# Attention of the last sequence: one more place for other matmuls in each step, 19 instead of 12 VectorE portions per pair

## The chip, the core and the metric

The kernel runs on one core of one Trainium2 chip. TensorE (PE) does matmuls and transposes into PSUM, VectorE (DVE) and ScalarE (ACT) read PSUM and work in SBUF, GpSimd (POOL) and SyncE (SP) mostly issue DMAs. The engines run their own instruction queues in order and wait for each other through semaphores. The metric is the device time of one execution in microseconds; the time before is the median of seven runs.

## The reference

Two layers, each with a sequence mixer and a mixture of experts, on 4 sequences of 1024 tokens of 256 values:

```python
x = L0_attn_x
x = x + _L0_attn_ref(_layernorm(x), ...)   # a gated recurrence (scan)
x = x + _L0_ffn_ref(_layernorm(x), ...)    # 8 experts, 2 per token
x = x + _L1_attn_ref(_layernorm(x), ...)   # causal attention, 16 heads of 64
x = x + _L1_ffn_ref(_layernorm(x), ...)    # 32 experts, 4 per token, and a shared one
return x
```

The change touches the third line, and the parts of the fourth that are computed beside it:

```python
att = jnp.einsum('bhcq,bhCq->bhcC', q, k) / d_query
att = jnp.where(causal, att, -jnp.inf)
p = jax.nn.softmax(att, axis=-1)
y = jnp.einsum('bhcC,bhCv->bhcv', p, v)
z = jnp.einsum('dvh,bhcv->bcd', W, y) * (math.sqrt(d_embed / d_value) / num_heads)
...
_, idx = jax.lax.top_k(scores + bias[None, :], K)      # routing of the fourth line
...
h = jax.nn.silu(jnp.einsum('ecd,edi->eci', xe, W1)) * jnp.einsum('ecd,edi->eci', xe, W3)
ye = jnp.einsum('eci,eid->ecd', h, W2)
```

## The kernel before

The attention runs sequence by sequence (`b` from 0 to 3), and in each over eight **pairs** of heads (`p`). A pair is cut into six **units**, the groups of 128-row query tiles in `GROUPS`: (0, 1), (2, 3), 4, 5, 6, 7. All 192 units form one pipeline in `run_steps`, whose order on all engines is written out by hand (`tc.manual_schedule()`): step `s` does the scores of unit `s` (L1452), the row minima on VectorE (L1466 and L1468) and the exponentials on ScalarE (L1481), the transposes of the exponentials of unit `s-1` (L1502, copied out at L1523), and the products with the values of unit `s-2` (`weighted`, L1538).

Between portions of `weighted`, each step has up to three **places** in the list `side` for a piece of other matmuls. Some hold what the attention itself needs: the queries, keys and values of the next pair (`queries`, `values`), and the softmax's divisors of the pair before (`norm_T`, `norm`). The others are called `"beside"` and take the next piece of a list of jobs, if that piece is due.

These jobs are Python generators (class `Beside`). `yield "pe"` announces a piece of matmuls and `yield "post"` the instructions that read its PSUM bank; `yield "dve"` ends a portion of VectorE work. A place calls `piece()`, which does something only when the job has come to a `"pe"`. At the end of each step, `beside.tick()` is called `TICKS[g]` times, and each call runs the job on to its next `yield`, if it stands at a `"dve"`. So places that meet a job at a `"dve"` stay empty, and so do calls that meet it at a `"pe"`. `TICKS` is (2, 3, 1, 3, 2, 1): 12 calls a pair.

In the last sequence (`b` = 3, pairs 24 to 31 when pairs are counted through all sequences) the jobs are, in order:

- `l3_out(2)`: the output projection of sequence 2, eight pieces `pz`, read at L1429;
- `l4_route(2, 0)` and `l4_route(2, 1)`: layer norm (L912, L913, the root in L884 to L897, `xn_l` at L919), transposes (`pt_l`, L931, copied by ScalarE at L935), gate scores (`pl_l`), top 4 (L947 to L967), positions (`pos_l`), rows (`row_l`, L1003), 16 scatters of rows to `xs_d` by GpSimd, the shared expert's hidden values (`s_l`), and the gates (L1034 to L1046);
- `l4_shared(2, h)`: the shared expert's second matmul (`sy`), added at L1061;
- `l4_experts_beside`: twelve tiles of experts' rows, two at a time. It makes the list of tiles (L1066 to L1097), loads rows (`room<-xs_d` on SP, L1112) and weights (`w_pairs<-e_w_dram` on POOL, L1107), then for two tiles each: rows on VectorE (L1117 to L1133), transposes `pta` (L1223, copied at L1225), hidden values `pea` (ScalarE L1210, VectorE L1211 and L1212), output `pya` (copied by ScalarE at L1195 into one buffer) and two scatters to `yt_d` (L859, POOL). Its weights go where the attention's weights of a pair stood, so it waits (`ready`) until those pairs are done: the first tiles until pair 28, from the second two on until pair 30.

All buffers in PSUM come from two pools: seven rotating banks (`ps_s`) for scores, transposes and pieces, and one for `weighted`.

After the last step, outside of the handwritten order, the output projection of sequence 3 (`pz`), what is left of the jobs, and `l4_route(3, 0)` and `l4_route(3, 1)` follow; their order on each engine is found by the scheduler:

```python
with tc.manual_schedule():
    run_steps()
drain(l3_out(B - 1, ps_s, "s"))
while beside.jobs or beside.job is not None:
    beside.step()
late = []
for h in range(2):
    drain(l4_route(B - 1, h, sm, ps_s, "s", late))
```

Then the last stage gathers the experts' rows of the first three sequences (`yg<-yt_d`, 24 loads on SP, L1729), adds them with their gates (L1736), runs the four tiles of experts that were not done beside (`ptg`, `eh`, `ey`, L1796 to L1820), gathers the last sequence's rows and stores. Its SBUF is that of the attention, so its loads come after the last reader of the attention's buffers.

Of the kernel before, what the change touches and what calls it, by code (L numbers as in the profile page):

```python
# [24 lines left out]
B, S, D = 4, 1024, 256  # L25
# [31 lines left out]
def block_kernel(  # L57
# [841 lines left out]
    def mm2(out, lhsT, rhs, start, stop):  # L899

        for par in range(2):
            r = slice(par * DH, (par + 1) * DH)
            nc.tensor.matmul(out[r], lhsT[:, r], rhs, start=start, stop=stop)  # L903
# [364 lines left out]
    with ExitStack() as ph:  # L1268
# [39 lines left out]
        def w_cols(k, p):  # L1308

            return w_pairs[:, p - 1, k] if p else w_pair0[:, k]  # L1310
# [4 lines left out]
        qs, ks, vs, ls, ys = {}, {}, {}, {}, {}  # L1315
        GROUPS = [(0, 1), (2, 3), (4,), (5,), (6,), (7,)]
        NG = len(GROUPS)
        TICKS = (2, 3, 1, 3, 2, 1)
        units = [(b, p, g) for b in range(B) for p in range(NP) for g in range(NG)]
        NU3 = len(units)  # L1320

# [31 lines left out]
        def values(b, p, hf):  # L1353

            held = {}

            def pe():
                held[0] = pv = ps_s.tile([P, HT, P], F32, name=f"pv_{b}_{p}_{hf}", tag="s")
                for q in range(HT):
                    i = hf * HT + q  # L1360
                    for c in range(NC_):
                        mm2(
                            pv[:, q, :], xTs[b][:, c, i * P : (i + 1) * P],
                            w_cols(2, p)[:, c, :], c == 0, c == NC_ - 1,
                        )

            def post():
                if hf == 0:
                    vs[b, p] = mid.tile([P, NT, P], F32, name=f"v_{b}_{p}", tag="v")
                nc.vector.tensor_copy(vs[b, p][:, hf * HT : (hf + 1) * HT, :], held[0])  # L1370

            return pe, post
# [47 lines left out]
        def l3_out(b, ps, tag):  # L1420
            y = [ys.pop((b, p)) for p in range(NP)]
            for i in range(NT):
                yield "pe"
                po = ps.tile([P, D], F32, name=f"pz_{b}_{i}", tag=tag)
                for p in range(NP):
                    mm2(po, y[p][:, i * P : (i + 1) * P], wo_t[:, p, :], p == 0, p == NP - 1)
                yield "post"

                nc.vector.scalar_tensor_tensor(  # L1429
                    x[b][:, i, :D], po, 0.0625, x[b][:, i, :D], ALU.mult, ALU.add  # L1430
                )
# [4 lines left out]
        def score_banks(u):  # L1436

            b, p, g = units[u]
            for par in range(2):
                for k, (i, kc) in enumerate(parts(u)):  # L1440
                    sps[u, k, par] = ps_s.tile(
                        [P, 512], F32, name=f"ps_{b}_{p}_{i}_{kc}_{par}", tag="s"
                    )
# [135 lines left out]
        beside = Beside()  # L1579
# [9 lines left out]
        def run_steps():  # L1589
            added, pending = [], []  # L1590
            at_pair = [0]
            inst = None
            for s in range(NU3 + 3):
                su = s if s < NU3 else None
                tu = s - 1 if 1 <= s <= NU3 else None
                vu = s - 2 if s >= 2 else None
                pair, g = divmod(s, NG)
                b, p = divmod(pair, NP)
                here, before = (b, p), divmod(pair - 1, NP)
                at_pair[0] = pair  # L1600
                ahead = divmod(pair + 1, NP)

                if g == 2 and p == 0 and 0 < b < B:
                    beside.jobs.append(l3_out(b - 1, ps_s, "s"))
                if (g, p) == ((2, 0) if b else (0, 4)) and b + 1 < B:
                    beside.jobs.append(l3_prepare_pieces(b + 1, sm, ps_s, "s"))
                if g == 2 and p == 0 and 0 < b < B:
                    beside.jobs += [l4_route(b - 1, h, sm, ps_s, "s") for h in range(2)]
                    beside.jobs += [l4_shared(b - 1, h, ps_s, "s") for h in range(2)]
                    if b == B - 1:  # L1610
                        beside.jobs.append(
                            l4_experts_beside(
                                sm, ps_s, "s", lambda j: w_pairs[:, j],
                                lambda j: at_pair[0] >= (B - 1) * NP + min(j, 5) + 1,
                            )
                        )

                side = []
                more = ahead[0] < B
                if g == 0:  # L1620
                    side = ["beside", "beside"]
                elif g == 1:
                    side = [norm_T(*before) if pair else "beside", "beside", "beside"]
                elif g == 2:
                    side = [
                        norm(*before, 0) if pair else None,
                        queries(*ahead, 0, False) if more else None,
                        norm(*before, 1) if pair else None,
                    ]
                elif g == 3:  # L1630
                    side = [queries(*ahead, 1, False), queries(*ahead, 0, True), "beside"] if more else []
                elif g == 4:
                    side = [queries(*ahead, 1, True), values(*ahead, 0), "beside"] if more else []
                else:
                    side = [values(*ahead, 1) if more else None, "beside", "beside"]
                side += [None] * (3 - len(side))

                def matmuls(k):

                    piece = side[k]  # L1640
                    if piece == "beside":
                        piece = beside.piece()
                    if piece is not None:
                        piece[0]()
                        pending.append(piece[1])

                def readers():
                    while pending:
                        pending.pop(0)()


                if tu is not None:
                    transposes(tu, 0)
                    transposed_out(tu, 0)
                if su is not None:
                    if g == 0:
                        ls[here] = sm.tile([P, NT, 2, 2], F32, name=f"l_{b}_{p}", tag="l")
                    score_banks(su)
                    scores(su, 0)
                    scores(su, 1)  # L1660
                if tu is not None:
                    transposes(tu, 1)
                if su is not None:
                    for par in range(2):
                        minimum(su, 0, par)
                        minimum(su, 1, par)
                    exps(su, 0, 0)
                    exps(su, 1, 0)
                if tu is not None:
                    transposed_out(tu, 1)  # L1670

                nb = GROUPS[units[vu][2]][-1] + 1 if vu is not None and vu < NU3 else 0
                cuts = [-(-nb // 2), nb, nb] if side[2] is None else [-(-nb // 3), -(-2 * nb // 3), nb]
                done = 0
                for k in range(3):
                    matmuls(k)
                    if cuts[k] > done:
                        weighted(vu, range(done, cuts[k]))
                        done = cuts[k]
                    if k == 0 and g == 0 and pair:  # L1680
                        norm_parts(*before)
                    if k == 0 and su is not None:
                        exps(su, 0, 1)
                        inst = exps(su, 1, 1)
                    readers()
                if nb:
                    weighted_out(vu)
                for _ in range(TICKS[g]):
                    beside.tick()
                if s % NG < NG - 1 and 2 <= s // NG * (NG - 1) + s % NG < TT + 2:  # L1690
                    l4_zeros(s // NG * (NG - 1) + s % NG - 2, inst)
                if 3 <= s < len(later) + 3:
                    added.pop(0)()
                if 1 <= s <= len(later):
                    added.append(later[s - 1](inst, sm))
            while pending:
                pending.pop(0)()

        with tc.manual_schedule():
            run_steps()  # L1700
# [13 lines left out]
    with ExitStack() as ph:  # L1714
# [107 lines left out]
        def l4_tiles(j0, n, lst):  # L1822
# [16 lines left out]
        more = nc.values_load(  # L1839
            flag_i[0:1, 0:1], min_val=0, max_val=1 << 20,  # L1840
            skip_runtime_bounds_check_because="a count, limited",
        )
# [87 lines left out]
```

## Time and profile before

| | us |
|---|---|
| median of 7 runs | 2043.13 (2040.6 to 2045.9) |
| the profiled execution, its own time | 2049.74 |
| its span in the profile | 2048.1 |
| layer 0, before the first score matmul | 609.2 |
| sequence 0, pairs 0 to 7 | 282.4 |
| sequence 1, pairs 8 to 15 | 339.9 |
| sequence 2, pairs 16 to 23 | 341.1 |
| sequence 3, pairs 24 to 31 and three more steps | 348.6 |
| the output projection of sequence 3 | 27.9 |
| from there to the end | 99.1 |

The stretches are read off the timeline: a sequence begins with its first score matmul (L1452). The places carry little in sequence 0, where there is nothing to do beside but the layer norm of sequence 1. How to read the rows that follow further down: a window's row has its bounds, its length, then for each engine the busy time and the number of instructions, the granted TensorE clock as a share of full speed, and the DMA engines' share and rate. A line of the chain of waits has a start, a length, and what the end of the execution hung on in that time. In a group of instructions, "out<-in" are the program's names of tiles, and what stands behind the bar is busy time, mean duration, and idle time of the engine before them.

### The profile page before, as it was taken

Reading aid. Unit: us, or ns where it says so; the run is one execution under the profiler, and the core shown is the slowest. Engines: PE = TensorE matmul, PEld = TensorE weight load, DVE = VectorE, ACT = ScalarE, POOL = GpSimd, SP = SyncE. Lnnn points to the kernel's source line nnn. Section 1 sums busy time; section 2 is a strip of 40 time slices with the busy share of each in tenths; the row PEclk is TensorE's granted clock in tenths of the full one; section 3 lists DMA queues with packets and bytes.
Section 4 is the critical chain, followed back from the end, with each engine's and each line's share of the span. In section 5 each row is a group of like instructions: output and inputs, shape, how many; then the busy total and the mean of one; then the engine's idle time right before and its main releaser. Section 6 shows DMA issues by size and latency. Waiting matters only on the chain.

```text
span 2048.1 us, 45184 instructions
## 1 busy us (share of the span) xinstructions
PE 1847.4 (90%) x17612; PEld 1209.0 (59%) x17612; DVE 1253.6 (61%) x4101; ACT 960.2 (47%) x2486; POOL 268.5 (13%) x307
## 2 busy tenths in 40 slices
PE   5679899999999999999998999989999999998963
PEld 2436466665656666666665666655666665666642
DVE  6686322244327776755677675676777477777666
ACT  3354122222236665663555654456555355655210
POOL 0334400022003200000003030000303003031022
PEclk8577999999999999999999999999999999999986
DMA  9122211122125433100000000000000000002135
GB/s 349 40 65 77 93 42 47 47 78 75 57 87 160 144 121 110 64 1 2 1 2 23 2 2 2 1 2 2 2 1 2 2 2 2 2 2 69 43 124 186
DMA packets 87151, 109.23 MB, mean 53 GB/s; under 512 B 13838, under 2 KB 76650, under 8 KB 85776
## 3 DMA queue, kind: packets, MB, share of 16 engines
q1 hardware_dynamic: 66528, 73.41, 10.9%
q0 software_dynamic: 15168, 27.05, 4.4%
q10 hardware_dynamic: 5232, 5.78, 0.8%
q8 instruction: 143, 2.34, 0.5%
q14 instruction: 80, 0.66, 0.1%
HBM read 51.75 MB, written 64.77 MB: 57 GB/s over the span
## 4 chain that ended last, share of the span: by engine, by line
PE 52%; DVE 12%; ACT 3%; DMA 2%; issue 1%; SPq 0%; POOL 0%; DVEq 0%; ACTq 0%; POOLq 0%
PE ps L1452 10%; PE pa L1538 9%; PE pt L1502 7%; PE pq L903 6%; PE pz L903 5%; PE pk L903 5%; PE pv L903 5%; DVE ps L1468 3%; ACT pe L1481 3%; DMA xs_d<-x,row_l 1%; PE s_l L903 1%; DVE pT L1523 1%; DVE nm L1466 1%; PE sy L903 1%; PE pb L1409 0%
## 5 line engine op out<-in xcount | busy, mean ns | idle before, releaser
L1481 ACT ACTIVATE pe<-ps,nm 128x512 f32<-128x512 f32 (+3 forms) x768 | 439.5, 578 | 287.1 <-DVE nm L1468 282.3
L1538 PE MATMUL pa<-pT,v 128*64 128x128 f32 (+1 forms) x4096 | 326.1, 292 | 0.0
L1538 PEld LDWEIGHTS pa<-pT,v 128*64 128x64 f32 x4096 | 245.0, 139 | 103.1 <-issue 84.7
L1452 PE MATMUL ps<-k,q 64*128 64x512 f32 (+3 forms) x1536 | 296.6, 502 | 0.0
L1502 PEld LDWEIGHTS pt<-ident,pe 64*128 64x128 f32 x4608 | 206.1, 140 | 115.3 <-issue 54.2
L1502 PE MATMUL pt<-ident,pe 64*128 64x64 f32 x4608 | 240.9, 230 | 29.1 <-ACT pe L1481 28.6
L608 PE MATMUL ph<-w_t,xgT 128*128 x544 | 258.6, 617 | 7.0 <-DVE hid L614 5.8
L1523 ACT COPY pT<-pt 128x512 f32<-128x512 f32 (+2 forms) x384 | 179.4, 520 | 165.7 <-PE pt L1502 164.0
L1466 DVE TENSOR_REDUCE nm<-ps 128x1 f32<-128x512 f32 x256 | 175.9, 687 | 122.6 <-PE ps L1452 121.5
L859 POOL DMA_INDIRECT xs_d<-x,row_l x104 | 103.2, 992 | 1038.1 <-DVE second L1011 988.0
L1523 DVE COPY pT<-pt 128x256 f32<-128x256 f32 (+3 forms) x384 | 178.4, 506 | 0.0
L1452 PEld LDWEIGHTS ps<-k,q 64*128 64x128 f32 x1536 | 134.3, 190 | 67.1 <-issue 54.0
L1468 DVE CUSTOM_DVE_ANT_0 ps<-ps,mask_a,nm 128x128 f32<-128x128 f32 (+3 forms) x256 | 143.2, 559 | 40.5 <-DVE nm L1466 8.5
L608 PEld LDWEIGHTS ph<-w_t,xgT 128*128 128x128 f32 x544 | 101.1, 197 | 110.3 <-issue 102.6
L1481 ACT ACTIVATION_READ_ACCUMULATOR pe<-ps,nm 128x1 f32 x768 | 152.1, 198 | 0.0
L903 PE MATMUL pq<-l_xT,w_pairs 128*64 128x512 f32 x448 | 114.8, 636 | 31.8 <-ACT pe L1481 31.8
L1468 DVE CUSTOM_DVE_ANT_0 ps<-ps,mask_a 128x128 f32<-128x128 f32 (+3 forms) x256 | 119.9, 518 | 25.6 <-PE ps L1452 23.6
L903 PE MATMUL pz<-wo_t,y 128*64 128x256 f32 x1024 | 115.0, 379 | 0.0
L903 PE MATMUL pv<-w_pairs,l_xT 128*64 128x128 f32 x1792 | 108.9, 274 | 2.9 <-ACT pe L1481 2.9
L628 PE MATMUL py<-w_t,hidT 128*128 x464 | 109.6, 379 | 0.0
L903 PE MATMUL pk<-l_xT,w_pairs 128*64 128x512 f32 x448 | 107.2, 599 | 0.5 <-ACT pe L1481 0.5
L680 POOL DMA_INDIRECT yg<-yq_d,back x64 | 60.6, 947 | 337.1 <-issue 234.2
(412 smaller groups left out, 2232.3 us busy)
## 6 DMA issues: line engine op xcount, KB each, us to landing
yt_d<-zeros SPq DMA_DIRECT2D x32, 512.0 KB, 3.2
xg<-xe_d SPq DMA_DIRECT2D x68, 129.0 KB, 2.1
yq_d<-ys SPq DMA_DIRECT2D x68, 128.0 KB, 2.0
xs_d<-zeros SPq DMA_DIRECT2D x65, 131.5 KB, 2.3
w_t<-w_dram SPq DMA_DIRECT2D x8, 1024.0 KB, 15.0
w_pairs<-e_w_dram POOLq DMA_DIRECT2D x12, 384.0 KB, 3.6
x<-x_in_dram SPq DMA_DIRECT2D x8, 512.0 KB, 8.2
w_t<-w_dram SPq DMA_DIRECT2D x8, 512.0 KB, 13.7
```

The source lines that it names most:

```text
L608: nc.tensor.matmul(pt, xgT[:, c, :], w[:, c, k * H0 : (k + 1) * H0], start=(c == 0), stop=(c == NC_ - 1),)
L628: nc.tensor.matmul(py, hidT[:, c, :], w[:, c, :], start=(c == 0), stop=(c == H0 // P - 1))
L680: gather = nc.gpsimd.indirect_dma_start(out=yg, out_offset=None, in_=yq_d[: rows * P, :], in_offset=bass.IndirectOffsetOnAxis(ap=back_i[:, ...
L859: i = nc.gpsimd.indirect_dma_start(out=self.out, out_offset=bass.IndirectOffsetOnAxis(ap=idx, axis=0), in_=src, in_offset=None, bounds_che ...
L903: nc.tensor.matmul(out[r], lhsT[:, r], rhs, start=start, stop=stop)
L1452: nc.tensor.matmul(t[:, :n], qs[b, p][rows, i * P : (i + 1) * P], ks[b, p][rows, kc * 512 : kc * 512 + n], start=True, stop=True,)
L1466: nc.vector.tensor_reduce(m[:, 0:1], t, AX.X, ALU.min)
L1468: nc.vector.tensor_tensor_reduce(out=t[:, :n], in0=t[:, :n], in1=mask[:, 512 - n :], scale=1.0, scalar=-LOWEST if kc == 0 else m[:, 0:1], ...
L1481: inst = nc.scalar.activation(pe[:, :n], sps.pop((u, k, par))[:, :n], AF.Exp, bias=ms[u, i, par][:, 1:2], scale=-1.0, accum_out=ls[b, p][: ...
L1502: nc.tensor.transpose(pts[u][r][:, j, par, :], pes[u, k, par][rows, j * P : (j + 1) * P], ident[rows, rows],)
L1523: copy(to, pts[u][r][:, :n])
L1538: nc.tensor.matmul(pas[0][rows, cols], vs[b, p][:, j, rows], pTs[u][:, j, par, a * P :], start=(j == 0), stop=(j == nb - 1),)
```

## The change

In the last sequence every step gets one more place `"beside"`, and two more in the last pair, where nothing is to be computed for a next pair. `TICKS_LAST` has 19 calls a pair there instead of 12. The portions of `weighted` are cut for as many places as there are; where there are three, as before. `side.append` stands ahead of the filling with `None`, so the first step of a pair, which had two places, has three there. The three steps behind the last pair are counted as a fifth sequence by `divmod` and stay as they were.

```diff
@@ -1315,7 +1315,9 @@
         GROUPS = [(0, 1), (2, 3), (4,), (5,), (6,), (7,)]
         NG = len(GROUPS)
+
         TICKS = (2, 3, 1, 3, 2, 1)
+        TICKS_LAST = (4, 4, 2, 4, 3, 2)
...
                 else:
                     side = [values(*ahead, 1) if more else None, "beside", "beside"]
+                if b == B - 1:
+                    side.append("beside")
+                    if not more:
+                        side.append("beside")
                 side += [None] * (3 - len(side))
...
                 nb = GROUPS[units[vu][2]][-1] + 1 if vu is not None and vu < NU3 else 0
-                cuts = [-(-nb // 2), nb, nb] if side[2] is None else [-(-nb // 3), -(-2 * nb // 3), nb]
+                n_cuts = 2 if side[2] is None else len(side)
+                cuts = [min(-(-(k + 1) * nb // n_cuts), nb) for k in range(len(side))]
                 done = 0
-                for k in range(3):
+                for k in range(len(side)):
                     matmuls(k)
...
-                for _ in range(TICKS[g]):
+                for _ in range((TICKS_LAST if b == B - 1 else TICKS)[g]):
                     beside.tick()
```

What a place takes is decided when the program is built, so the new order can be counted out. In the last sequence, with what is left at the end of a step, the jobs stand so (pairs counted through all sequences):

| job | before | after |
|---|---|---|
| `l3_out(2)` | 24 to 25, second step | 24 to 25, first step |
| `l4_route(2, 0)` | 25 to 27, second step | 25 to 26, third step |
| `l4_route(2, 1)` | 27 to 29, fourth step | 26 to 27, fifth step |
| `l4_shared(2, h)` | 29 to 30, first step | 27 to 28, first step |
| expert list | 30, second step | 28, second step |
| first two tiles | transposed in 30 | transposed in 28 |
| tiles 2 to 11 | from 31; `pea` of the third two and all later ones left over | 30 to 31, second step |
| left for after the steps | 4 `pea`, 3 `pta` and 4 `pya` | nothing |

The engines' instructions are the same in number but for a few on TensorE (8789 rows in the old order's listing, 8795 in the new one's).

## The prediction

> **What bounds the kernel now.** I read the page, then stretches of the last sequence, then single steps of it, then the chain of waits through the tail. Pairs are counted through all sequences, so the last sequence has pairs 24 to 31, of six steps each. The page says that TensorE is the engine to watch up to about slice 37, at full clock, and no longer behind it:
>
> ```profile
> PE 1847.4 (90%) x17612; PEld 1209.0 (59%) x17612; DVE 1253.6 (61%) x4101; ACT 960.2 (47%) x2486; POOL 268.5 (13%) x307
> PE   5679899999999999999998999989999999998963
> PEclk8577999999999999999999999999999999999986
> ```
>
> In the stretches below, a step runs from the first score matmul (L1452) of one unit to that of the next. The rows are pair 7 (nothing beside it), then pairs 27 and 30, pair 31 with the three steps behind it, the output projection `pz` of sequence 3, the expert pieces left over, and the rest. Columns: us; busy time of PE, PEld, DVE, ACT, POOL; granted clock; DMA.
>
> ```profile
> 857.44:891.57 34.13, 33.49 (x433) 22.87 (x429) 22.36 (x64) 23.31 (x66) 0.00 (x0) 1.00 0.01 2
> 1712.78:1753.78 41.00, 36.10 (x432) 23.70 (x429) 32.15 (x108) 23.23 (x66) 4.26 (x5) 0.96 0.01 1
> 1836.45:1881.07 44.62, 39.50 (x487) 26.67 (x485) 32.11 (x99) 23.72 (x67) 3.26 (x6) 0.92 0.22 67
> 1881.07:1921.18 40.11, 33.86 (x477) 25.23 (x473) 29.20 (x95) 23.76 (x68) 3.76 (x6) 1.00 0.14 41
> 1921.18:1949.03 27.85, 27.85 (x262) 18.61 (x262) 13.38 (x52) 0.20 (x1) 2.74 (x3) 1.00 0.13 39
> 1949.03:1968.01 18.98, 13.01 (x173) 10.53 (x169) 11.45 (x49) 3.30 (x7) 7.26 (x8) 1.00 0.35 101
> 1968.01:2048.10 80.09, 33.53 (x214) 22.19 (x212) 54.25 (x221) 8.37 (x21) 16.45 (x18) 0.70 0.53 174
> ```
>
> A bare pair is TensorE from end to end (33.49 of 34.13). Pair 27 has 7 us more but only 2.6 us more TensorE: its VectorE portions hold up the scores. Single steps show how: second and third step of bare pair 7; second step of pair 18; third step of pairs 29 and 30; fifth step of pair 25.
>
> ```profile
> 860.77:865.14 4.37, 4.37 (x67) 3.28 (x65) 4.16 (x18) 2.84 (x9) 0.00 (x0) 1.00 0.00 0
> 865.14:871.11 5.97, 5.33 (x70) 2.98 (x67) 4.04 (x11) 4.32 (x14) 0.00 (x0) 1.00 0.02 4
> 1332.66:1340.31 7.65, 4.79 (x65) 3.41 (x65) 7.17 (x31) 2.85 (x10) 0.00 (x0) 1.00 0.00 0
> 1805.08:1814.26 9.18, 6.66 (x70) 3.32 (x67) 6.56 (x21) 3.89 (x12) 6.95 (x7) 0.81 0.03 2
> 1845.86:1858.13 12.27, 7.15 (x70) 3.49 (x67) 9.22 (x32) 4.30 (x14) 3.10 (x6) 0.72 0.45 139
> 1657.24:1664.39 7.15, 7.15 (x99) 4.98 (x96) 5.45 (x16) 4.39 (x12) 0.00 (x0) 1.00 0.00 0
> ```
>
> VectorE has 0.2 us to spare in a bare second step: of 3.0 us of portions issued at the end of pair 18's first step, 2.86 appear as idle TensorE. Portions issued after a second step come through but for 0.7 to 1.1: the list (L1066 to L1097, 1846.24 to 1851.47, 5.2 us) leaves 5.12 of idle in pair 30, 0.64 of them there in a bare pair too. Portions after a fourth step cost little: 3.1 us before the last row cost nothing. So **where** a portion falls decides its price.
>
> In the tail, the chain of waits passes through the leftover expert pieces into the routing of sequence 3, whose ScalarE copies to `xT_l` are queued behind theirs:
>
> ```profile
> 1957.47 2.52 DMA room<-xs_d
> 1966.26 4.29 DMA yt_d<-room,to_i_a
> 1970.65 0.59 ACT room L1195
> 1971.24 0.99 ACT xT_l L935 x2
> 1972.27 1.03 PE pl_l L903 x28
> ```
>
> **What the change does, part by part.** Counted out place by place: before, four hidden matmul groups (`pea`), three transposes (`pta`) and four outputs (`pya`) are left when the steps end. Afterwards the list of jobs is empty by the second step of pair 31. The routings of sequence 2 move from pairs 25 to 29 into 25 to 27, the expert list from pair 30 to 28; pair 29 has nothing beside it, since the weights' places are still held by the attention.
>
> *Out of the tail.* The h=0 transposes of the last routing start right behind `pz`, not at 1968.01: 18.98 us. ScalarE no longer waits for a scatter ahead of their copies. Before, L949 of h=0 came 5.6 us after its transposes began (1973.64); in h=1 the copy began 0.75 after them and `pl` was done 2.9 after them, so 3.4 will do: 2.2 us. Given back: VectorE used to do the h=1 statistics between expert pieces; now the new order has them among the h=0 operations (ten of 0.1 to 0.2, four `xn` of 0.35, L1028 of 0.69 ahead of `row_l`). That adds up to 3.2 us at the h=1 transposes and 2.4 at the h=1 scores. Scatters, 24 gathers `yg` (SP issued them right behind the h=1 transposes, at 1984.16) and the last four expert tiles follow in the old order. **Tail: 18.98 + 2.2 - 2.4 = 18.8 us shorter.** 16, if the interleaving costs double; 24, if the last scatters land 5 us sooner (issued up to 2003.33, with a median landing of 3.2, yet SP's next loads went at 2012.53, behind the gathers' traffic).
>
> *Into the steps: TensorE.* Eleven pieces by durations in the chain: four of 1.75, three of 0.6, four of 0.86: 12.2 us. Their DMAs come earlier with them (a weight load of 384 KB, a row load and a scatter of 1.0 us of POOL for each of the six tiles); nothing on POOL or SP in that stretch waits behind them but each other.
>
> *Into the steps: stalls.* Prices of portions by rows: statistics of a tile 0.61 (L912, L913), root 3.8 (19 operations 0.2 apart), `xn` 0.35, score portions 1.2, 0.9, 0.9 and 1.0, gate sums 1.2, a gate 0.87, rows of an expert tile 0.95. Time over 34.13 before, pairs 24 to 30: 15.5, 15.5, 6.8, 6.9, 5.5, 8.9, 10.5, together 69.6. After:
> - 24: seven outputs of 3.45, two shared pieces of 0.87: 25.9.
> - 25: matmuls 5.8; root and two `xn` pairs after the second step (5.2) cost 4.1; three score portions after the fifth and one behind it 3: 13.
> - 26: matmuls 4.0; 1.65 after the first step cost 1.5, 3.8 (sums, three gates) after the second 2.7, 4.6 (root, `xn`) after the fifth 3.3, as in pair 27, where 3.9 cost 1.9 in the sixth step and more behind it: 11.5.
> - 27: matmuls 8.1; four score portions (4.0) after the first step, partly under 2.4 of matmuls, 3; others 1: 12.1.
> - 28: as pair 30 before, with two more row portions: 11.
> - 29: 0.
> - 30: matmuls 10.0, row portions 3: 13.
>
> Together 86.5: **+16.9 us.** Pair 31: the first step has 3.3 of new matmuls, and 3.4 of VectorE come through with 1.8; the second has 2.4 more matmuls, 1.2 of waiting for the hidden values that its last place reads at once, and 1 where ScalarE waits for the scatters of the copy before (these copies were 4.6 and 6.5 apart in the tail); behind that wait stand its exponentials, and for them TensorE's transposes. Saved further on: 3.2. **+6.5 us.** Steps: 23.4 longer. Below, +9: pieces alone, 3 of them in pair 31's idle time. Above, +32: see the third rival.
>
> *Clock.* It was 0.81 on average in the 9.18 row (2.52 of idle), 0.72 in the 12.27 row, and a `pq` there took 3.68 us where its like took 1.9: 1.8 lost. Pair 25's third step gets a gap of some 4.7; I add half of such a loss, 0.8.
>
> The Trainium skill speaks against this change here: "TensorE: Matmul & The Clock Gate", "HAM oscillation — how this bites in real kernels", has the clock halved by idle gaps of more than about 3.4 us. By that bound the gap in pair 25 loses the whole 1.8 and the 9.18 row should not have lost any, which it did; the sum by the rule would be +6.4 instead of +5.4.
>
> **Sum.** 23.4 + 0.8 - 18.8 = +5.4 us. The profiled execution took 2049.74 us (span 2048.1), 6.6 above the median of the runs, 2043.13; both should move alike. **2048.5 us**, and 2055 for an execution like the profiled one.
>
> **Rivals.**
> 1. *The portions hide.* More pieces in a step give VectorE cover, or the last scatters land sooner: steps +13, tail -20, so -7: 2036 us. For it: the 7.15 row. Against it: the added portions go to first and second steps above all. It decides where the steps cost less than 14.7 (18.8 less the bound below).
> 2. *Even.* Half of the extra stalls, steps +18, tail -18: 2043.
> 3. *Stalls breed.* The clock halves behind three or four gaps of 2.5 us and more (1.8 each), and pair 31 waits twice as long for its scatters: steps +31, tail -17: +14, 2057.
> 4. *The places stay empty*, held back by their own portions. Counting the sequence out, the list does run dry; no share.
>
> **How the numbers follow.** Measurements of this kernel tell about 0.2% (4 us) from no change. Forecast, +4 to +10 (2047 to 2053): 0.41. First: 0.23. Second: 0.20. Third: 0.16. So slower 0.57, same 0.20, faster 0.23. The bounds (steps +9 to +32, tail -24 to -16) span 2028 to 2059; the low end needs both at their best, so I keep 2035 to 2058.
>
> **What would show it.** Right: no `room` rows behind `pz`; `pz` starting near 1945; the last routing's transposes directly behind it; the end 105 to 111 us after the start of `pz` (126.9 before); pair 25's third step near 10 us, pair 29 at 34.1, ScalarE's L1195 waiting for `yt_d` in pair 31. Wrong: `pz` before 1936, or a tail over 112 us because gathers or scatters, not the routing, end last.

## The result, and the profile after

After took **2056.13 us** (median of 18 runs, 2051.95 to 2067.57), beside 2042.56 for before (45 runs). The ratio is 1.0064, with a 95% interval of 1.0053 to 1.0075: some 13 us slower. The forecast was 2048.5, so the sign held and the size was more than doubled; the time lies in the range, next to the third rival's 2057.

First the page of after: busy time by engine, TensorE in 40 slices, the granted clock.

```profile
PE 1859.5 (90%) x17612; PEld 1211.3 (59%) x17612; DVE 1252.9 (61%) x4101; ACT 959.7 (47%) x2486; POOL 269.6 (13%) x307
PE   5579899999999999999989999999999988899873
PEclk9578999999999999999999999999999999999986
```

The work is the same, instruction for instruction. TensorE is busy 12.1 us longer for it, which a slower clock can give and more work cannot, and three weak slices (8, 8, 8) stand where pairs 25 to 28 run, which had 9 throughout before.

Next the stretches, with columns as before: pairs 25, 28, 29 and 30, pair 31 with the three steps behind it, the output projection `pz`, and the rest.

```profile
1635.70:1683.33 47.63, 42.33 (x505) 27.19 (x501) 32.39 (x115) 24.43 (x69) 0.00 (x0) 0.93 0.01 1
...
1778.84:1827.38 48.54, 42.82 (x487) 27.43 (x485) 33.54 (x106) 23.60 (x67) 2.73 (x5) 0.89 0.15 46
1827.38:1861.81 34.43, 33.79 (x431) 22.60 (x429) 22.36 (x64) 23.29 (x66) 0.53 (x1) 1.00 0.05 14
1861.81:1908.16 46.35, 43.97 (x564) 30.68 (x561) 29.93 (x90) 26.22 (x72) 9.66 (x12) 1.00 0.31 94
1908.16:1956.91 48.75, 39.12 (x516) 29.40 (x513) 29.54 (x95) 24.89 (x70) 5.99 (x6) 0.96 0.05 15
1956.91:1984.69 27.78, 27.78 (x259) 18.33 (x257) 12.48 (x46) 0.16 (x1) 0.00 (x0) 1.00 0.01 1
1984.69:2063.80 79.11, 35.07 (x214) 22.63 (x212) 56.73 (x243) 7.88 (x20) 14.78 (x16) 0.70 0.52 175
```

The stretch of 18.98 us with the leftover expert pieces is gone: `pz` runs straight into the last routing. From the start of `pz` to the end it is 106.9 us (27.78 + 79.11), where it was 126.9: **20.1 shorter**. From the first score matmul of pair 24 to `pz` it is 381.5 us (1575.43 to 1956.91), where it was 348.6: **32.9 longer**. The difference is 12.8 us; 2.8 more of the two profiles' difference lie ahead of pair 24, where the programs are alike.

Pair 29 is bare (34.43), while pairs 25 and 28 are 13.5 and 14.4 us over the bare 34.13. Single steps of after show what they lose: the third steps of pairs 25 and 28, the fourth of pair 28, and the fourth of pair 30, which has a like load.

```profile
1646.91:1659.40 12.49, 7.86 (x70) 3.53 (x68) 8.95 (x34) 4.32 (x14) 0.00 (x0) 0.73 0.00 0
1788.25:1801.65 13.40, 8.28 (x71) 3.94 (x68) 10.40 (x35) 4.29 (x14) 2.21 (x4) 0.76 0.46 140
1801.65:1813.61 11.96, 11.76 (x100) 6.40 (x100) 4.54 (x15) 5.27 (x14) 0.00 (x0) 0.84 0.08 23
1881.08:1890.90 9.82, 9.82 (x107) 6.00 (x104) 3.17 (x10) 5.86 (x15) 1.66 (x2) 1.00 0.14 42
```

A bare third step has 5.97 us and 5.33 of TensorE. The two third steps have 6.5 and 7.4 more, part of it idle (4.6 and 5.1) and part busy at a clock of 0.73 and 0.76. The fourth step of pair 28 has hardly any idle time, and is still 2.1 longer than its like at full clock. TensorE's timeline of after, through the gap in pair 28 and out of it:

```profile
1790.19 0.65 PE L1540 MATMUL pa<-pT,v 128*64 128x256 f32 x4
1795.96 3.68 PE L903 MATMUL pq<-l_xT,w_pairs 128*64 128x512 f32 x8 [5.12 <-ACT pe L1483]
...
1801.65 2.88 PE L1454 MATMUL ps<-k,q 64*128 64x512 f32 x8
```

The `pq` of eight instructions takes 3.68 us in place of 1.9, and six microseconds after the gap the scores still take 2.88, where those of the other fourth steps of this sequence take 1.51: the clock is granted at half speed from 1795.3 for 10.2 us.

### The profile page after: what moved, and what is told of

It reads as the page before. It is cut to its first block, busy times and chain, and to the rows that moved or that the text cites. A ratio compares the mean times of both kernels' runs of the same rounds, so it can differ in the third digit from the quotient of the medians.

```text
span 2063.8 us, 45182 instructions
## 1 busy us (share of the span) xinstructions
PE 1859.5 (90%) x17612; PEld 1211.3 (59%) x17612; DVE 1252.9 (61%) x4101; ACT 959.7 (47%) x2486; POOL 269.6 (13%) x307
## 5 line engine op out<-in xcount | busy, mean ns | idle before, releaser
L1470 DVE CUSTOM_DVE_ANT_0 ps<-ps,mask_a,nm 128x128 f32<-128x128 f32 (+3 forms) x256 | 143.2, 559 | 41.3 <-DVE nm L1468 8.0
L1470 DVE CUSTOM_DVE_ANT_0 ps<-ps,mask_a 128x128 f32<-128x128 f32 (+3 forms) x256 | 119.7, 518 | 22.6 <-PE ps L1454 20.7
L903 PE MATMUL pv<-w_pairs,l_xT 128*64 128x128 f32 x1792 | 109.0, 275 | 4.6 <-ACT pe L1483 4.6
```

The lines of the kernel that those rows point to most:

```text
L1470: nc.vector.tensor_tensor_reduce(out=t[:, :n], in0=t[:, :n], in1=mask[:, 512 - n :], scale=1.0, scalar=-LOWEST if kc == 0 else m[:, 0:1], ...
```

## The experiments

All are edits of after, unless said otherwise. "Steps" is the time from the first score matmul of pair 24 to `pz`, "idle" is TensorE's idle time in it, "half" the time in it at half the clock, "tail" the time from `pz` to the end; these four come from one profiled execution each. The ratio is that of the timed runs to those of before on the same chip, and the times of before beside it show how far one chip and one session are from another.

| kernel | steps | idle | half | tail | time | before | ratio, 95% interval |
|---|---|---|---|---|---|---|---|
| before | 348.6 | 24.7 | 17.1 | 126.9 | | 2042.6 | |
| after | 381.5 | 36.5 | 27.3 | 106.9 | 2056.1 | 2042.6 | 1.0064 (1.0053 to 1.0075) |
| places only | 358.9 | 20.9 | 17.1 | 110.1 | 2037.6 | 2043.0 | 0.9982 (0.9966 to 0.9998) |
| portions only | 369.4 | 36.0 | 27.3 | 116.0 | 2056.9 | 2043.0 | 1.0063 (1.0042 to 1.0084) |
| portions moved | 372.9 | 33.3 | 13.7 | 106.1 | 2050.7 | 2043.0 | 1.0031 (1.0014 to 1.0047) |
| gaps filled | 373.9 | 28.7 | 6.8 | 108.0 | 2049.0 | 2043.0 | 1.0035 (1.0017 to 1.0052) |
| one place in the last pair | 376.0 | 35.9 | 17.1 | 105.4 | 2054.4 | 2045.4 | 1.0041 (1.0026 to 1.0056) |
| first steps back | 375.4 | 33.7 | 17.1 | 106.7 | 2053.5 | 2045.4 | 1.0035 (1.0018 to 1.0052) |
| places, list in three | 357.1 | 21.8 | 10.2 | 111.4 | 2037.6 | 2045.4 | 0.9970 (0.9953 to 0.9986) |
| the same, gaps filled | 360.1 | 20.5 | 17.1 | 109.0 | 2037.9 | 2045.4 | 0.9965 (0.9951 to 0.9978) |
| dense to pair 28 | 376.8 | 35.4 | 20.5 | 104.8 | 2053.6 | 2043.9 | 1.0040 (1.0021 to 1.0058) |
| dense from pair 30 | 367.9 | 28.3 | 17.1 | 107.4 | 2047.3 | 2043.9 | 1.0011 (0.9995 to 1.0027) |
| dense in pair 31 | 359.3 | 21.3 | 10.2 | 105.8 | 2038.9 | 2047.1 | 0.9969 (0.9949 to 0.9989) |
| dense in 31, list in three | 398.7 | 41.7 | 47.8 | 107.5 | 2171.6 | 2174.4 | 0.9979 (0.9968 to 0.9990) |

**Places or portions?** One run keeps the places and goes back to 12 portions, one the other way round.

```diff
-        TICKS_LAST = (4, 4, 2, 4, 3, 2)
+        TICKS_LAST = (2, 3, 1, 3, 2, 1)
```

> The new places, with the old 12 portions per pair in the last sequence. Counted out, two of the eleven matmul groups (a hidden group and an output) are then still left behind the steps. Before took 2042.6 us, after 2056.1. Theory A (bunched VectorE portions open idle gaps on TensorE, and the clock halves behind them; the places themselves cost only their matmuls): nine groups come in, 11 us by their times in the steps, some 1 of waiting in pair 31, the tail is about 17 shorter, gaps and half-clock time stay as before (24.7 and 17 us in the last sequence): 2036 to 2041. Rival B (the places cost, each dependent piece waits for the one before it in the same step): the steps get some 27 longer, sum about 2051 to 2055.

```diff
-                if b == B - 1:
-                    side.append("beside")
-                    if not more:
-                        side.append("beside")
```

> The 19 portions per pair in the last sequence, without the new places. Counted out, five of the eleven matmul groups are left behind the steps. Theory A: six groups come in, 7 us, the tail is 11 to 12 shorter, and the bunched portions cost the 12 us of gaps and about 6 of clock that after has over before: 2052 to 2058, and half-clock stretches of 20 us or more in the last sequence. Rival B (the places are what costs): 7 and 1 us of steps against 11 to 12 of tail, 2037 to 2041, half-clock time as before (17 us).

Measured: 2037.6 and 2056.9, both where theory A had them. The windows of steps and tail of the run with the places only, then of the one with the portions only:

```profile
1566.90:1925.79 358.89, 338.01 (x4055) 227.56 (x4051) 244.69 (x792) 194.03 (x545) 46.83 (x52) 0.98 0.08 22
1925.79:2035.92 110.13, 64.30 (x510) 43.09 (x508) 71.50 (x291) 9.07 (x23) 18.32 (x20) 0.80 0.39 129
```

```profile
1571.37:1940.78 369.41, 333.39 (x4011) 227.09 (x4008) 241.92 (x780) 193.22 (x543) 44.54 (x50) 0.96 0.07 21
1940.78:2056.81 116.03, 68.46 (x554) 46.22 (x552) 74.42 (x302) 9.98 (x25) 20.61 (x22) 0.80 0.37 123
```

The places bring nine of the eleven groups into the steps and 16.8 us out of the tail, and add 10.3 to the steps, with less idle time than before (358.89 - 338.01 = 20.9). The portions bring in only six groups and have 36.0 of idle. So the loss comes with the portions, and the places alone make the kernel faster than before, if only by 0.2%, with an interval that ends at 0.9998. The second hit says less than it seems: 9.84 us of those 36.0 are a single gap in pair 30, the longest of all runs, and 13.7 us of half clock follow it. TensorE of that run:

```profile
1850.04 0.89 PE L1540 MATMUL pa<-pT,v 128*64 128x128 f32 x12
1860.76 1.12 PE L1223 MATMUL pta<-ident,room 128*128 128x128 f32 x4 [9.84 <-ACT pe L1483]
```

The theory had no such gap; its cause is shown below, with the runs that are dense in some pairs only.

**Where in the pair?** The theory was that portions behind the first and second step cost, and those behind the third and fourth do not. Two runs put that to the test: the same 19 moved there, and the added ones behind the first and second taken back.

```diff
-        TICKS_LAST = (4, 4, 2, 4, 3, 2)
+        TICKS_LAST = (2, 2, 6, 6, 2, 1)
```

> After, with its 19 portions per pair of the last sequence issued as 2, 2, 6, 6, 2, 1 in place of 4, 4, 2, 4, 3, 2: behind the third and fourth step, where the next step has VectorE time to spare. Counted out, nothing is left behind the steps, as in after. Theory A: matmuls 14 us in, tail 20 shorter, gaps no more than before (the list still leaves one of 5 us), half-clock time 17 us or less: 2033 to 2040. Rival B: the pieces are the same, so 2051 to 2056. Rival C (the total of VectorE work, not its place, decides): 2054 to 2058.

```diff
-        TICKS_LAST = (4, 4, 2, 4, 3, 2)
+        TICKS_LAST = (2, 3, 2, 4, 3, 2)
```

> After, with 16 portions per pair in the last sequence: 2 behind the first step in place of 4 and 3 behind the second in place of 4, as before; the added portions behind the third to sixth steps stay. Nothing is left behind the steps. Theory A in its narrow form (the portions bunched behind first and second steps are the cost): idle TensorE in the last sequence falls from 36.5 us to 24 to 27, half-clock time to 17 or less, 2040 to 2046. Rival F (every added portion costs alike): three of seven are taken back, 2056 less 8, so 2047 to 2050 or more. In the run with the portions moved behind the third and fourth step, six at once overran those steps too (gaps of 3.2 in the fourth and fifth steps); here there are two and four.

Both missed what the theory wanted. The run with the portions moved took 2050.7, just under rival B's range. The run with 16 portions took 2053.5; its ratio of 1.0035 is 2049.7 on before's 2042.6, as rival F had it. Both ratios lie clear of after's, so some 6 us of the 13 went, and with them half-clock time (13.7 and 17.1 us in place of 27.3). But the idle time is 33.3 and 33.7, barely under after's. In the first, the gaps have only moved. Pair 25's fourth step and pair 26's fifth, by the timeline of that run:

```profile
1653.32 0.60 PE L1540 MATMUL pa<-pT,v 128*64 128x256 f32 x4
1657.22 1.94 PE L903 MATMUL pk<-l_xT,w_pairs 128*64 128x512 f32 x8 [3.29 <-ACT pe L1483]
```

```profile
1706.69 0.61 PE L1540 MATMUL pa<-pT,v 128*64 128x128 f32 x8
1710.50 2.83 PE L903 MATMUL pv<-w_pairs,l_xT 128*64 128x128 f32 x24 [3.20 <-ACT pe L1483]
```

Those steps wait for the exponentials in the same way as the third step of pair 28 did: the root and both pairs of `xn` came behind the third step of pair 25, the gate sums, four gates and a tile's statistics behind the fourth of pair 26. A step that takes three portions for nothing does not take six. **The theory that the place in the pair alone decides fell here**, and with it the reading in the prediction that portions behind a fourth step cost little; that holds for the number seen before.

**Which pairs?** Idle time was 33 to 36 us in every run with more than 12 portions per pair (but where matmuls fill the gaps, see below), and 21 in those with 12 and the places. So the next theory: the same VectorE work is pressed into fewer pairs, and pair 29 stands empty. Two runs make only some pairs dense, a third follows one finding.

```diff
-                for _ in range((TICKS_LAST if b == B - 1 else TICKS)[g]):
+                for _ in range((TICKS_LAST if 24 <= pair < 29 else TICKS)[g]):
```

> After, with its 19 portions per pair in pairs 24 to 28 alone and the old 12 in pairs 29 to 31. Routings and list still run in pairs 25 to 28, pair 29 still has nothing beside it, and nothing is left behind the steps. So far every run with more than 12 portions per pair had 33 to 36 us of idle TensorE in the last sequence, wherever in the pair they stood, and those with 12 had 21 to 25. Theory H (the cost is that the same VectorE work is pressed into fewer pairs, while pair 29, with time to spare, stands empty): idle 31 to 36, and 2048 to 2054. Rival I (the cost is in pairs 30 and 31, where pieces that need each other's results follow in one step): idle 22 to 26, and 2038 to 2043.

The other two have `30 <= pair < 32` and `pair == 31` in that place.

> After, with the old 12 portions per pair up to pair 29 and 19 in pairs 30 and 31 alone. Routings then use pairs 25 to 29 and the list falls to pair 30, as before; counted out, nothing is left behind the steps. Theory H: idle 21 to 26 us in the last sequence, half-clock time 17 or less, the tail 105 to 108: 2036 to 2042, about as the places alone. Rival I: idle 30 or more, 2047 to 2053.

> The last run's kernel with pair 30 back to 12 portions: 19 in pair 31 alone. In that run a gap of 7.45 us stood in pair 30's second step: owner, list and the first rows were all issued behind the first step, and the rows held VectorE for 3.15 us, waiting for the load that the list had just started, ahead of the masks that TensorE was waiting for. Here the rows fall behind the second step again; nothing is left behind the steps. Theory J (that bunch cost pair 30 some 4 us of gap and 2 of clock): the gap is 3.3 again, idle 23 to 25 in the last sequence, 2037 to 2042. Rival I (pieces that need each other, in the last pair): 2045 to 2049, with no gap over 3.5.

Dense to pair 28: 2053.6 and 35.4 us of idle, as theory H had it. Routings, list and first tiles take the pairs 25 to 30 in both; that run has 26.4 us of idle TensorE in these, the run with the places only 14.1. (Length of a pair less TensorE's busy time, pair by pair: 5.3, 6.8, 5.3, 6.0, 0.6 and 2.4, against 1.4, 1.8, 1.4, 2.6, 2.1 and 4.9.) TensorE's longest gaps in the third steps of pairs 25, 26 and 28 are after's to 0.02 us. Pairs 25 to 28 of the run dense to pair 28, then of the one with the places only:

```profile
1632.22:1821.34 189.12, 165.71 (x1938) 105.95 (x1936) 137.99 (x473) 97.56 (x273) 34.41 (x37) 0.95 0.05 14
```

```profile
1627.17:1790.20 163.03, 155.88 (x1868) 102.03 (x1864) 122.49 (x421) 96.97 (x272) 30.79 (x32) 0.98 0.01 2
```

Dense from pair 30 was to be 2036 to 2042 and took 2047.3, with 28.3 us of idle: a miss for theory H, and at the lower edge of rival I's time. Part of it is a mechanism that neither had. VectorE and then TensorE of that run, in pair 30's second step:

```profile
1842.13 0.23 DVE L1097 TENSOR_SCALAR slotl_key_a<-list_key_a,slot_no 128x12 f32<-128x12 f32 x1
1845.50 0.41 DVE L1117 TENSOR_SCALAR room<-room 128x256 f32<-128x256 f32 x1 [3.15 <-DMA room<-xs_d]
...
1846.39 0.57 DVE L1470 CUSTOM_DVE_ANT_0 ps<-ps,mask_a 128x384 f32<-128x384 f32 x1
```

```profile
1847.78 0.36 PE L1504 MATMUL pt<-ident,pe 64*128 64x64 f32 x1 [7.45 <-ACT pe L1483]
```

With four portions behind the first step, the list and the first tile's rows came in one bunch. The rows need the load that the list has just started, VectorE stood still for 3.15 us until it landed, and the masks of the next scores (L1470) stood behind it in VectorE's queue. The gap of 9.84 in the run with the portions only is the same bunch with a second tile's rows in it (VectorE waits of 3.12 and 0.80 for the loads).

That run also shows that theory H is too narrow. Without the places its jobs cannot run ahead, and the routings and the shared expert fill pairs 25 to 29 much as before. Over these five pairs before and this run have nearly the same VectorE work (150.6 and 151.7 us), but 12.7 and 20.0 us of idle TensorE. Before, then the portions only:

```profile
1622.20:1836.45 214.25, 201.60 (x2404) 134.17 (x2401) 150.62 (x498) 120.52 (x338) 31.65 (x32) 0.98 0.01 2
```

```profile
1620.98:1844.53 223.55, 203.51 (x2425) 134.99 (x2421) 151.68 (x505) 120.31 (x338) 31.57 (x32) 0.98 0.01 2
```

So portions that are bunched behind single steps cost some 7 us in the same pairs. Nor is it the empty pair 29 that costs: with the portions moved, and with the first steps back, the expert list falls into pair 29 (43.95 and 43.90 us long), and the idle time is 33 us all the same. What the runs with 33 us or more share is more than three portions behind some step of pairs 25 to 28. How much of the loss is the bunch and how much the fewer pairs, they do not say.

With pair 30 back at 12 portions that bunch is gone, and only pair 31 is dense: 2038.9, ratio 0.9969, idle 21.3 (under the expected 23 to 25), the largest gap 3.32 again. Pair 31 alone can be dense at no cost that shows, and all of the tail's groups come in (tail 105.8).

The bunch is only part of the 8 us between the last two runs. Pairs 30 and 31, dense from pair 30 and then dense in pair 31 alone:

```profile
1833.11:1883.22 50.11, 41.62 (x511) 28.49 (x509) 33.43 (x106) 24.76 (x69) 6.49 (x10) 0.93 0.29 86
1883.22:1938.62 55.40, 46.00 (x605) 35.55 (x601) 35.50 (x117) 26.59 (x74) 12.44 (x14) 0.94 0.20 61
```

```profile
1835.38:1881.69 46.31, 41.66 (x511) 28.61 (x509) 33.38 (x106) 24.75 (x69) 6.51 (x10) 0.96 0.31 93
1881.69:1932.21 50.52, 44.37 (x604) 33.19 (x600) 35.18 (x117) 26.45 (x74) 10.48 (x12) 0.97 0.22 66
```

Pair 30 is 3.8 us longer in the first, the cost of the bunch; pair 31, with the same pieces in both, is 4.9 longer, 3.2 of them idle. In the first one `pea` and one `pya` wait 2.1 and 2.3 us for the results they need, where they wait 0.2 and 0.8 in the other run. That is rival I's cost, of some 3 us.

**The clock.** Is the half clock behind the gaps a cost of its own? The next run leaves all gaps' causes in place and lets TensorE repeat the first product of `weighted` in three of them, `again` times by the list `WARM` (pair and step, counted from 0).

```diff
+        WARM = {(25, 2): 7, (26, 2): 4, (28, 2): 8}
...
+            for n in range(2 * again):
+                rows = slice(n % 2 * DH, (n % 2 + 1) * DH)
+                nc.tensor.matmul(
+                    pas[0][rows, 0 : 2 * P], vs[b, p][:, 0, rows], pTs[u][:, 0, n % 2, :],
+                    start=True, stop=True,
+                )
             for j in blocks:
```

> After, with extra matmuls that TensorE runs in three of its idle gaps (third steps of pairs 25, 26 and 28: the first product of the weighted sum is done 7, 4 and 8 times more, into the same place, before it is done for good). The gaps themselves and all VectorE work stay. Theory A, its clock half: the half-clock stretches behind these gaps (6.8, 3.4 and 10.2 us) do not come, which saves 1.8 in pair 25, 1.2 in pair 26 and 3.9 in pair 28, some 6 to 7 us: 2048 to 2051. Rival D (the half-clock stretches cost nothing that the gaps do not cost anyway, or come from something else than the idle gaps): 2055 to 2057, or more where the extra matmuls delay the step.

Measured 2049.0, ratio 1.0035, as theory A had it: some 6 us of the 13 come back (1.0064 - 1.0035, of 2042.6; 2 to 10 by the two intervals). TensorE in pair 28's third step, where L1539 is the repeated product:

```profile
1777.47 3.67 PE L1539 MATMUL pa<-pT,v 128*64 128x256 f32 x32
1780.97 0.60 PE L1548 MATMUL pa<-pT,v 128*64 128x256 f32 x4
1783.25 1.94 PE L903 MATMUL pq<-l_xT,w_pairs 128*64 128x512 f32 x8 [1.67 <-ACT pe L1483]
...
1786.36 1.51 PE L1454 MATMUL ps<-k,q 64*128 64x512 f32 x8
```

The wait ends as late as before, but `pq` takes 1.94 in place of 3.68 and the scores 1.51 in place of 2.88. Of the 27.3 us of half clock 6.8 are left, none of them behind the three filled gaps.

**The last pair's second place.**

```diff
                 if b == B - 1:
                     side.append("beside")
-                    if not more:
-                        side.append("beside")
```

> After, with one new place per step in the last pair in place of two; all else as in after. Counted out, the last output falls into the third step of pair 31 in place of the second, and still nothing is left behind the steps. Theory A: the output that reads the hidden values at once no longer stops TensorE (1.0 us in pair 31's second step), and it fits into the idle time of the third: 2053 to 2056, 1 to 3 us under after. Rival E (the second place of the last pair is what made the steps longer than forecast): 2046 to 2050.

2054.4, but before took 2045.4 beside it, and the ratio is 1.0041, whose interval overlaps after's by a little. Idle time is 35.9, as in after; half-clock time is 10 us less, 6.8 of that behind the same gap of 5.12 in pair 28, which this edit does not touch (in the run dense to pair 28, too, that gap was followed by 3.4 us of half clock and not by 10.2). I take from it that the second place is not the main cause, and leave open whether it costs 1 or 4 us.

**A better version.** The gap of 3.32 behind the expert list in the run with the places only can be cut: `yield "dve"` behind the first and the second of the list's three large operations (each 0.95 us).

```diff
+        yield "dve"
         rows = None
...
+        yield "dve"
         t = l4s.tile([P, 16], F32, name=f"list_{nm}", tag="list")[:, :n]
```

> The places alone (12 portions per pair), with the experts' list of 5.2 us issued as three portions in place of one. The run with the places alone had 2037.5 us and a gap of 3.32 in pair 30's second step, behind the list. Theory A: one part of 0.95 falls behind the first step of pair 30, the others (3 us) behind the second, which has about 1 us to spare; the gap of 3.32 goes, one of about 2 comes in the third step, and less half-clock time behind it: 2034 to 2037. Rival G (the list is late then, and the expert tiles with it): 2038 to 2041.

> The same, and TensorE's gaps of 1.4 to 2.5 us in the third steps of pairs 11, 13, 15, 19, 23 and 25 filled with repeated matmuls (4, 3, 5, 4, 5 and 3 times), which change no result. In the runs before, 24 to 27 us of half clock lie in the sequences 0 to 2. Theory A: at least the stretches behind these gaps go, some 10 us of half clock, 3 to 5 us of time: 2030 to 2034. Rival D (gaps under 3 us have no part in the half clock): as the run with the list in three, or 1 us more.

> The new places, 19 portions in pair 31 alone, and the list in three portions: the two parts that gave the least time so far put together. From the runs: the list in three took the gap behind it from 3.32 to 2.23 us (357.1 us of steps against 358.9), and 19 portions in pair 31 took the last two groups out of the tail (105.8 against 110.1) for 0.4 us of steps. If the two add, 3 to 5 us under the places alone: 2033 to 2036, a ratio of 0.995 to 0.997. Rival K (what the last two groups give up in the tail comes back in the steps, and the rest is within the measurement): 2037 to 2040.

The gap went to 2.23 and into the third step, as said, but the ratio (0.9970) cannot be told from that of the places only (0.9982). Filling further gaps of 1.4 to 2.5 us brought nothing that shows (0.9965), and there was little to win: without the filling, half clock followed one of these six gaps in the profile, that in pair 11. Rival D is not shown by this, for gaps of that size do lose clock at times: behind the 2.52 us in pair 15 there were 3.4 us of it in the run with the places only, and none with the list in three. The last run came on a chip on which both kernels take 6% longer; 0.9979 there does not say that the two parts add. What stands: the places with 12 portions, with or without 19 in pair 31, are 0.2 to 0.3% faster than before, and 0.8 to 0.95% faster than after.

## Why the prediction was right in sign and short in size

Its terms in order, with what after's profile has in their place:

- **Tail, -18.8:** -20.1. No `room` row stands behind `pz`, and the transposes `pt_l` follow it at 1984.69 without a pause. The end came 106.9 after the start of `pz`, within the 105 to 111 named.
- **Matmuls of the moved pieces, +12.2:** 13.7 at full clock. In before's steps two `pea` groups had 3.8 us, so four are 7.6 and not 7.0; a `pya` is 1.05 and not 0.86 (2.1 for two), four 4.2; three `pta` 1.9.
- **Stalls, +11.2** (23.4 less the 12.2): idle TensorE in the steps rose from 24.7 to 36.5, by 11.8. The sum was right, its places less so: pair 25's third step was to be near 10 us and is 12.49, with a gap of 4.63 as foreseen ("some 4.7") and the rest clock. Pair 29 came as forecast (34.4).
- **Clock, +0.8: this is the term that was far too small.** In the stretches granted half the clock, TensorE was busy for 24.3 us in after's steps of the last sequence, and for 13.3 in before's; half of the difference, **5.5 us**, is the loss. I charged pair 25's gap half of one slow `pq` and took pair 28 over from pair 30 with its old loss, while the half clock lasted 6.8 us behind the one and 10.2 behind the other, through the scores and into the next step. This is one execution of each kernel, 9.3 us above after's median and 7.2 above before's, and such stretches vary: the 10.2 were 3.4 in two other runs with the same gap in pair 28. But the timed runs with the gaps filled measured such a loss by themselves, some 6 us.
- What is left, 1.9 us of busy time (32.9 - 13.7 - 11.8 - 5.5), I cannot place.

So 12.8 in place of 5.4: the clock 4.7 over its term, matmuls 1.5, stalls 0.6, the unplaced 1.9, less 1.3 by which the tail is shorter than forecast. By pair, the steps' 9.5 us over the forecast lie in pair 28 (14.4 over the bare pair, forecast 11), 27 (14.7, forecast 12.1), 31 (8.6 over before's, forecast 6.5) and 26 (12.6, forecast 11.5); the others came within 0.8. `pz` starts at 1956.9 and not near 1945, for the same reasons and the 2.8 us ahead of pair 24.

The third rival had the right mechanism for the clock (three or four gaps, 1.8 each) and the right time, the time partly by luck, for its other half is not there: in pair 31 no ScalarE copy waited for the scatters. ScalarE's waits in after from 1900 to 1957, by what released it:

```profile
ACT pe L1483 <- DVE nm L1470: 9.8, 7, 2.0
ACT room L1210 <- PE pea L903: 7.5, 3, 5.3
...
ACT room L1195 <- PE pya L903: 2.2, 1, 2.2
```

L1195, the copy, waited for its matmuls and not for a `yt_d`. What pair 31 lost stood elsewhere: `pea` needs the copy L1225 of the transposes, and VectorE, in its own order, did seven operations of the divisors first.

```profile
1909.63 0.66 PE L1223 MATMUL pta<-ident,room 128*128 128x128 f32 x4
...
1914.36 3.37 PE L903 MATMUL pea<-room,w_pairs 128*64 128x128 f32 x32 [2.13 <-issue]
```

```profile
1913.49 0.25 DVE L1387 CAST wb<-rl 128x16 bf16<-128x16 f32 x1
1913.57 0.68 DVE L1225 COPY room<-pta 128x512 f32<-128x512 f32 x1
```

The first rival's hope, that portions find cover, is not wrong as such; it came true for 12 portions a pair (idle 20.9, under before's 24.7), and not for 19. The second, half the stalls, has nothing for it. The fourth is out: the list of jobs did run dry.

The prediction took the routings' early end, in pair 27, for granted as part of the change and did not ask what it was good for. It was good for nothing: from the second two on, the expert tiles wait for pair 30, so pair 29 stood bare. With 12 portions up to pair 30 and 19 in pair 31, the routings end in pair 28, the list comes in pair 30, and still nothing is left behind the steps (2038.9 us).

## What to carry to other kernels

Work that is hidden beside a bound engine should come as thin as its deadline allows: a schedule that ends early in front of a fixed gate has only paid more per step. Count what a step can take, not whether it can take something, and keep a portion that waits for a load a step away from the one that starts it. And price a gap on TensorE with what it does to the clock: the gaps here were 11.8 us more, the slow matmuls behind them 5.5.

## What the runs showed of the hardware

The half clock comes in stretches of 3.41 us and multiples of it, and how many is not a matter of the gap alone: the gap of 5.1 us in pair 28 was followed by 10.2 us of half clock in after and by 3.4 in the runs dense to pair 28 and with one place in the last pair; 4.63 by 6.8, 7.45 by 6.8, 9.84 by 13.7, 3.32 by 3.4. Shorter gaps lost clock at times: 3.20 and 3.08 did, 3.29 (portions moved) did not, and the same gap of 2.81 in pair 27 did in the run with the gaps filled and did not in after. Stretches of 3.41 us also stand behind gaps of 2.13 (after, at 1914.7) and 1.49 (places only, at 1893.3), and some with no gap over 1.4 us in the 25 us before them (before, at 1754.9; after, at 1730.4). The Trainium skill, "TensorE: Matmul & The Clock Gate", section "HAM oscillation — how this bites in real kernels", puts the bound at about 3.4 us of idle time. All gaps above that lost clock in the last sequence, as it says; so did several below it, and here the measurement decides.

The same program ahead of pair 24 does not always take the same time: over the profiles of before, after and the variants that are alike up to there (but for the last run's chip), pair 24 begins between 1565.0 and 1576.0 us: at 1565.0 and 1565.4 where 126.3 us of half clock lie ahead of it, at 1575.4 and 1576.0 where 153.6 do. A single execution of this kernel is no measure of a change of 5 us. On the chip of the last run, stretches of 17.07 us of half clock came in steps without such gaps (at 1804.6, with none over 1.4 us since 1745), 150 us in all from the first score matmul to `pz`; what causes these was not tried.
